# CIN kernel: the V2 matmuls moved ahead of a product row, and all six writes of M issued from ScalarE

## The chip, the cores and the metric

The kernel runs on one core of a Trainium2 chip. The metric is the device time of one execution in microseconds (us); the times given for a kernel are those of several executions, and their median. The profile is of one execution.

The engines are named as in the profile: PE is TensorE (matmuls), PEld its weight loads, DVE is VectorE, ACT is ScalarE, POOL is GpSimd, SP is SyncE. "SPq" and "ACTq" are the instruction streams of SP and ACT where they issue DMAs.

## The reference

A compressed interaction network of three layers over `x` of shape (1024, 64, 16), that is batch B, feature F, embedding E. Each layer multiplies `x` with the layer before it, feature by feature, and contracts the 64 x 64 products with a weight:

```python
x0 = x
h = x
for i in range(3):
    z = jnp.einsum('bfe,bge->bfge', x0, h).reshape(B, 64 * fh, E)
    y = jnp.einsum('oc,bce->boe', Ws[i], z) + bs[i][None, :, None]
    if i != 2:
        x_i, h = y[:, :64], y[:, 64:]
    else:
        x_i, h = y, y
    xs.append(x_i)
out = jnp.sum(jnp.concatenate(xs, axis=1), axis=2) @ fc_w.T + fc_b
```

The last layer is only summed against `fc_w`, so its weight can be folded: with V2[f,g] = sum over o of fc2[o] * W2[o,f,g], and M = V2 contracted with the second half of W1, the third layer's share is a form in x, x and h1. Both h1 and this form ("q") are then contractions of the same products x_f * x_g, h1 with weights from W0, q with weights from M.

## The kernel before

**Tiles.** The batch is cut into 32 chunks of 32 rows; a chunk has N = 32 * 16 = 512 columns, and features lie along the partitions. A chunk's products are made as four "rows" j = 0 to 3. A row is one block `z` of 128 x 2048: `product(c, j)` multiplies `xa[c]` (four shifted copies of x, 128 x 4 x 512) with `xb[c][j]` (x shifted by the row's offset). Most rows are made on DVE (L240, 2.2 us each), some on POOL. `half_contract(c, j, ...)` then runs four matmuls for each row named, with the left half of `w_all` (the h1 weights), into the PSUM tile of chunk c. One such matmul shows as two records of PE.

**The head.** The first four chunks c0, c1, c2, c3 are chunks 2, 3, 0 and 1. Only their h1 half is contracted at first, since the right half of `w_all` (the q weights) comes from M, which the kernel computes itself at this point:

- V2: eight matmuls (L359) of `fv2` (fc2, broadcast) with the two halves of W2, into two PSUM tiles `pv`. DVE transposes each (L364), and DVE (L371) and ACT (L372) copy the result into `v2t`.
- M: eight matmuls (L387) of `v2t` with W1 into four PSUM tiles `pm`; ACT copies them into the block `m_sb` (L401).
- M goes to DRAM, into `md`, by six DMAs: two of 512 KB (L416, one from each half of the partitions), two of 256 KB (L419, L420), one of 32 KB (L421) and one of 28 KB (L422). They are called write 1 to write 6 below. In the kernel before, write 1 and writes 3 to 6 are issued by SP and write 2 by ACT.
- M is read back skewed, as rows (L469, `read_rows`) and columns (L463, `read_columns`), into the block `ms`: of the first row's reads one half of the partitions by SP, the other by ACT; the columns of rows 1 to 3 by SP alone. DVE adds rows and columns into the right half of `w_all` (L499, `q_weights(j)`).
- Then 32 matmuls (L281, `head_q_tile`) run the kept products of chunks 0 and 1 through the q weights, and everything after is driven by a list.

**What sets the order.** The kernel is under a manual schedule: each engine runs its instructions in the order in which the code issues them, and the later part of the kernel sorts a list of (time, job) pairs by hand-given times before issuing it. Waits are semaphore waits put in by the framework. DMAs take one of eight completion semaphores in turn, whichever engine issues them, and an issue waits until the semaphore's DMA before it has landed. Order in the code around the change, for the engines concerned:

- PE: the last columns of c0 (L257), row 0 of c1 (L248), V2 (L359), rows 3 and 1 of c1, M (L387), `pcx` (L396), row 2 of c1, rows 0 to 3 of c2, rows 0, 3, 1, 2 of c3 (L248), then L281.
- DVE: rows of c0, rows 0 and 1 of c1, the two transposes (L364), two copies (L371), row 2 of c1, rows 0 to 3 of c2, rows 0, 1, 2 of c3, then L499.
- ACT: two copies of `v2t` (L372), the copy of `xb` for row 3 of c2 (L398), the four copies of M (L401), write 2 (L416), the copies of `xb` for rows 0 and 1 of c3 (L430), `cx` (L432), h1 of c1 (L268, L269), six copies of x for the kept chunks (L175 to L177), its three reads of M (L469, L463, L469), h1 of c2 and of c3.
- SP: the loads of x and weights up to c3, `linear` (L343), writes 1 and 3 to 6, its reads of M, `va` (L493), the loads of chunks 4 and 5.

Of the kernel before, what the change touches and what calls it, by code (L numbers as in the profile page):

```python
# [42 lines left out]
F = 64  # L43
# [27 lines left out]
def cin_kernel(ctx, tc, xra, xrb, wh, w0r, w1h, w2t, wx1, wx0, vec, lin, out):  # L71
    nc = tc.nc
# [19 lines left out]
    def used(n, times=1):  # L92
        left[n] -= times
        assert left[n] >= 0
        if left[n] == 0:
            vacant.append(n)
# [21 lines left out]
    for base in (0, 64, -64):  # L118
        nc.gpsimd.affine_select(
            out=shift, in_=shift, compare_op=ALU.not_equal, fill=1.0, base=base,  # L120
# [65 lines left out]
    c0, c1, c2, c3 = HEAD  # L186
# [49 lines left out]
    def product(c, j, first=0, last=NI, engine=nc.vector, uses=1):  # L236
        if first == 0:
            zs[c, j] = take(uses)
        at = slice(first, last)
        engine.tensor_tensor(  # L240
            blocks[zs[c, j]][:, at, :], xas[c][:, at, :],
            xbs[c][j].unsqueeze(1).to_broadcast([128, last - first, N]), ALU.mult,
        )

    def half_contract(c, *js, last=None):
        for j in js:
            for i in range(NI):
                nc.tensor.matmul(  # L248
                    accs[c][halves[i % 2]], w_all[:, j * NI + i, 0:64], blocks[zs[c, j]][:, i, :],
                    start=(j == 0 and i < 2), stop=(j == last and i > 1),  # L250
                )
            used(zs[c, j])
# [70 lines left out]
    for i in range(NI):  # L323
# [20 lines left out]
        out=linear, in_=bass.AP(tensor=lin.tensor, offset=lin.offset, ap=[[0, 128], [1, 384]])  # L344
# [2 lines left out]
    product(c1, NJ - 1, engine=nc.gpsimd)  # L347
    for j in (0, 1):
        product(c1, j)
    half_contract(c1, 0)  # L350


    v2b = take()
# [18 lines left out]
        nc.scalar.copy(v2t[halves[1 - h], at], v2q[halves[h]])  # L372
    used(v2b)
    product(c1, 2)
    half_contract(c1, 3, 1)


    mb = take()
# [29 lines left out]
    row = EXT * F  # L408

    def m_ap(f1, f2, dims):  # L410
        return bass.AP(tensor=md.tensor, offset=md.offset + f1 * row + f2 * F, ap=dims)

    m_rows = m_sb.rearrange("p m c -> p (m c)")

    for half, queue in enumerate((nc.sync, nc.scalar)):
        queue.dma_start(  # L416
            out=m_ap(0, 32 * half, [[row, F], [1, 32 * F]]), in_=m_rows[halves[half]]
        )
    nc.sync.dma_start(out=m_ap(64, 32, [[row, 32], [1, 32 * F]]), in_=m_rows[64:96])  # L419
    nc.sync.dma_start(out=m_ap(32, 64, [[row, 32], [1, 32 * F]]), in_=m_rows[32:64])  # L420
    nc.sync.dma_start(out=m_ap(64, 64, [[row, 32], [1, 4 * F]]), in_=m_rows[0:32, 0 : 4 * F])  # L421
    nc.sync.dma_start(  # L422
        out=m_ap(64, 68, [[row, 4], [4 * F, 7], [1, 4 * F]]),
        in_=m_rows[0:4, 4 * F :].rearrange("p (k c) -> p k c", c=4 * F),
    )
# [695 lines left out]
```

## Time and profile before

| | |
|---|---|
| median of 3 runs | 448.4 us (447.93, 448.40, 448.61) |
| the profiled execution | 448.52 us, of which the profile's span covers 446.7 |
| PE busy | 441.9 us, 99% of the span |
| DVE busy | 393.5 us, 88% |
| POOL busy | 366.7 us, 82% |
| ACT busy | 117.2 us, 26% |
| DMA | 99.85 MB, mean 224 GB/s |

How to read it: the profile gives the start and the length of each instruction on each engine, and for an engine that sat idle the releaser, the event that ended the wait. Times count from the start of the span. A timeline merges neighbouring instructions of one kind into one line: the start of the first, the time that they took together, the line of the code, the tile written and those read, and the count. PE's records overlap, since matmuls are pipelined: two records of L248 start every 0.43 us and each is listed with about 0.59 us.

### The profile page before, as it was taken

The numbers are of one execution on the slowest core, as the hardware profiler recorded it, in microseconds if no ns is written. First come the engines' busy times: TensorE is split into PE (matmuls) and PEld (weight loads), VectorE is DVE, ScalarE is ACT, GpSimd is POOL, SyncE is SP. The second block draws the span as 40 slices with busy tenths as digits, with TensorE's granted clock in tenths as the row PEclk, the third lists the DMA queues.
The fourth block names the chain that finished last, engine by engine and source line by source line (L and its number), as shares of the span: only waits on it lengthen the run. The fifth ranks groups of instructions, "written<-read, shape, count | busy, mean of one in ns | idle before, by whom it ended". The sixth has DMA issues, their size and how long they took to land.

```text
span 446.7 us, 5944 instructions
## 1 busy us (share of the span) xinstructions
PE 441.9 (99%) x2234; PEld 151.8 (34%) x2234; DVE 393.5 (88%) x293; ACT 117.2 (26%) x215; POOL 366.7 (82%) x128
## 2 busy tenths in 40 slices
PE   9999999999999999999999999999999999999997
PEld 5333333333333333333333333333333333333345
DVE  4897699989989989999899979999899998999644
ACT  3163241332223123131312212231231313123211
POOL 5424788998997979799797979979797997979910
PEclk9999999999999999999999999999999999999999
DMA  8996998397949597694949769494976949692400
GB/s 299 416 343 151 331 412 342 93 346 133 357 117 295 167 221 273 137 360 102 303 158 234 268 128 357 105 312 149 232 264 133 372 92 286 223 240 86 98 1 0
DMA packets 35060, 99.85 MB, mean 224 GB/s; under 512 B 6389, under 2 KB 7189, under 8 KB 28441
## 3 DMA queue, kind: packets, MB, share of 16 engines
q1 hardware_dynamic: 32376, 84.90, 53.7%
q0 software_dynamic: 1872, 13.63, 17.4%
q10 hardware_dynamic: 784, 0.95, 0.8%
q8 instruction: 17, 0.28, 0.2%
q14 instruction: 11, 0.08, 0.0%
HBM read 84.20 MB, written 1.64 MB: 192 GB/s over the span
## 4 chain that ended last, share of the span: by engine, by line
PE 91%; DMA 6%; DVE 1%; SPq 0%; issue 0%; DVEq 0%
PE alpha L530 45%; PE delta L530 20%; PE beta L530 11%; PE acc L530 7%; PE q L530 3%; DMA xa<-in_xra 3%; PE acc L281 3%; DMA xb<-in_xrb 2%; PE acc L248 2%; DMA z<-in_w0r 1%; DVE z L240 1%; PE y L530 0%; SPq L145 0%; SPq L195 0%; PE hx L530 0%
## 5 line engine op out<-in xcount | busy, mean ns | idle before, releaser
L661 POOL TENSOR_TENSOR z<-z,z 128x2048 f32<-128x2048 f32 (+1 forms) x78 | 299.9, 3878 | 28.8 <-PE alpha L530 28.8
L530 PE MATMUL alpha<-z,ws 128*64 128x512 f32 x624 | 235.4, 593 | 0.0
L644 DVE TENSOR_TENSOR z<-xa,xp 128x2048 f32<-128x2048 f32 x103 | 231.5, 2279 | 1.2
L530 PEld LDWEIGHTS alpha<-z,ws 128*64 128x64 f32 x624 | 72.4, 137 | 91.0 <-issue 90.5
L530 PE MATMUL delta<-z,w_all 128*64 128x512 f32 x208 | 96.5, 592 | 0.0
L530 PE MATMUL alpha<-z,w_all 128*64 128x512 f32 x208 | 93.4, 593 | 0.0
L530 PE MATMUL beta<-z,w_all 128*64 128x512 f32 x208 | 92.7, 594 | 0.0
L530 PE MATMUL delta<-z,ws 128*64 128x512 f32 x208 | 91.4, 592 | 0.0
L558 ACT COPY xp<-xb 128x512 f32<-128x512 f32 x88 | 51.4, 587 | 127.4 <-DVE z L644 109.2
L240 DVE TENSOR_TENSOR z<-xa,xp 128x2048 f32<-128x2048 f32 (+1 forms) x29 | 45.5, 1619 | 4.3 <-ACT xp L558 3.2
L240 POOL TENSOR_TENSOR z<-xa,xb 128x2048 f32<-128x2048 f32 x6 | 28.2, 4760 | 17.5 <-DMA xb<-in_xrb 17.5
L530 PEld LDWEIGHTS delta<-z,w_all 128*64 128x64 f32 x208 | 28.4, 137 | 32.2 <-issue 32.2
L530 PEld LDWEIGHTS alpha<-z,w_all 128*64 128x64 f32 x208 | 28.1, 137 | 32.0 <-issue 29.5
L530 PEld LDWEIGHTS delta<-z,ws 128*64 128x64 f32 x208 | 28.5, 137 | 27.4 <-issue 25.7
L530 PEld LDWEIGHTS beta<-z,w_all 128*64 128x64 f32 x208 | 28.0, 137 | 27.4 <-issue 27.4
L530 PE MATMUL acc<-z,w_all 128*64 128x512 f32 x128 | 28.1, 592 | 0.0
L248 PE MATMUL acc<-z,w_all 128*64 128x512 f32 x96 | 21.6, 597 | 1.1 <-DVE z L240 1.1
L675 ACT ACTIVATE snap<-alpha,vs 64x512 f32<-64x512 f32 x13 | 8.9, 684 | 50.2 <-PE alpha L530 50.2
L682 DVE SCALAR_TENSOR_TENSOR snap<-alpha,vs,snap 64x512 f32<-64x512 f32 x13 | 9.7, 747 | 12.5 <-PE alpha L530 12.5
L672 ACT COPY snap<-alpha 64x512 f32<-64x512 f32 x13 | 7.6, 581 | 49.2 <-PE delta L530 34.9
L305 DVE TENSOR_REDUCE acc<-uu 128x64 f32<-128x1024 f32 (+2 forms) x19 | 19.6, 1036 | 0.2
L650 DVE TENSOR_TENSOR xp<-xp,xb 128x512 f32<-128x512 f32 x26 | 18.2, 699 | 0.8
(121 smaller groups left out, 357.6 us busy)
## 6 DMA issues: line engine op xcount, KB each, us to landing
xa<-in_xra SPq DMA_DIRECT2D x32, 1024.0 KB, 8.9
xb<-in_xrb SPq DMA_DIRECT2D x128, 256.0 KB, 8.5
z<-z POOLq DMA_DIRECT2D x13, 1024.0 KB, 8.1
e<-in_xra SPq DMA_DIRECT2D x28, 128.0 KB, 8.2
xx<-in_xra SPq DMA_DIRECT2D x28, 128.0 KB, 2.5
z<-in_w2t SPq DMA_DIRECT2D x2, 1024.0 KB, 8.4
z<-in_wx SPq DMA_DIRECT2D x2, 1024.0 KB, 9.9
xa<-in_xra SPq DMA_DIRECT2D x5, 256.0 KB, 4.3
```

The lines of the kernel that those rows point to most:

```text
L240: engine.tensor_tensor(blocks[zs[c, j]][:, at, :], xas[c][:, at, :], xbs[c][j].unsqueeze(1).to_broadcast([128, last - first, N]), ALU.mult,)
L248: nc.tensor.matmul(accs[c][halves[i % 2]], w_all[:, j * NI + i, 0:64], blocks[zs[c, j]][:, i, :], start=(j == 0 and i < 2), stop=(j == las ...
L281: nc.tensor.matmul(accs[c][halves[1 - c % 2]], w_all[:, t, 64:128], blocks[zs[c, j]][:, i, :], start=(t == 0), stop=False, skip_group_chec ...
L305: nc.vector.tensor_reduce(acc[rows, of, k, half], uu[rows, of if at is None else at, E * half.start : E * half.stop].rearrange("p k (b e) ...
L530: nc.tensor.matmul(out, w, rhs, start=start, stop=stop, skip_group_check=True)
L558: nc.scalar.copy(bank, xbs[c][j])
L644: engine.tensor_tensor(blocks[b], xas[c], xbs[c][j].unsqueeze(1).to_broadcast([128, NI, N]), ALU.mult)
L650: nc.vector.tensor_tensor(bank, bank, xbs[p["b"]][j], ALU.add)
L661: nc.gpsimd.tensor_tensor(*(blocks[b][:, first:last] for b in (o, x, y)), ALU.subtract if in1 == "T3" else ALU.add,)
L672: nc.scalar.copy(snaps[0][p["O"]], alpha(p))
L675: nc.scalar.activation(snaps[1][p["O"]], alpha(p), AF.Identity, bias=bh1[p["A"]])
L682: nc.vector.scalar_tensor_tensor(hb_, alpha(p), bh1[p["A"]], hb_, ALU.add, ALU.add)
```

## The change

Two edits. The matmuls of c1's row 0 are taken from ahead of V2 and put behind it, so that PE runs V2 right after c0's columns and then rows 0, 3 and 1 of c1. And all six writes of M are issued by ACT, one after the other, where SP issued five of them.

```diff
@@ -347,7 +347,6 @@
     product(c1, NJ - 1, engine=nc.gpsimd)
     for j in (0, 1):
         product(c1, j)
-    half_contract(c1, 0)
...
@@ -372,7 +371,7 @@
     used(v2b)
     product(c1, 2)
-    half_contract(c1, 3, 1)
+    half_contract(c1, 0, 3, 1)
...
@@ -412,14 +411,14 @@
-    for half, queue in enumerate((nc.sync, nc.scalar)):
-        queue.dma_start(
+    for half in range(2):
+        nc.scalar.dma_start(
             out=m_ap(0, 32 * half, [[row, F], [1, 32 * F]]), in_=m_rows[halves[half]]
         )
-    nc.sync.dma_start(out=m_ap(64, 32, [[row, 32], [1, 32 * F]]), in_=m_rows[64:96])
-    nc.sync.dma_start(out=m_ap(32, 64, [[row, 32], [1, 32 * F]]), in_=m_rows[32:64])
-    nc.sync.dma_start(out=m_ap(64, 64, [[row, 32], [1, 4 * F]]), in_=m_rows[0:32, 0 : 4 * F])
-    nc.sync.dma_start(
+    nc.scalar.dma_start(out=m_ap(64, 32, [[row, 32], [1, 32 * F]]), in_=m_rows[64:96])
+    nc.scalar.dma_start(out=m_ap(32, 64, [[row, 32], [1, 32 * F]]), in_=m_rows[32:64])
+    nc.scalar.dma_start(out=m_ap(64, 64, [[row, 32], [1, 4 * F]]), in_=m_rows[0:32, 0 : 4 * F])
+    nc.scalar.dma_start(
         out=m_ap(64, 68, [[row, 4], [4 * F, 7], [1, 4 * F]]),
         in_=m_rows[0:4, 4 * F :].rearrange("p (k c) -> p k c", c=4 * F),
     )
```

In the changed kernel every line from L350 on has a number lower by one. On ACT the six writes stand where write 2 stood: behind the copies of M and ahead of the copies of `xb` for c3. The counts of matmuls, products, copies and DMAs are the same. Some blocks `z` change places, since row 0 of c1 is released later: the reads of M land in a block that held W2, no longer in the one of c1's row 0.

## The prediction

> **What bounds the kernel now.** I read the page's busy times first.
>
> ```profile
> PE 441.9 (99%) x2234; PEld 151.8 (34%) x2234; DVE 393.5 (88%) x293; ACT 117.2 (26%) x215; POOL 366.7 (82%) x128
> ```
>
> PE is busy in all but 4.8 of 446.7 us. So only what makes PE wait, or takes a wait away, can move the end, and the waits lie in the first 43 us. The timeline of PE there:
>
> ```profile
> 17.56 1.94 PE L248 MATMUL acc<-z,w_all 128*64 128x512 f32 x8 [0.83 <-DVE z L240]
> 19.43 1.92 PE L359 MATMUL pv<-z,fv 128*32 128x512 f32 x16
> ...
> 26.80 8.88 PE L248 MATMUL acc<-z,w_all 128*64 128x512 f32 x40
> 35.94 7.09 PE L248 MATMUL acc<-z,w_all 128*64 128x512 f32 x32 [0.26 <-DVE z L240]
> 42.85 13.90 PE L281 MATMUL acc<-z,w_all 128*64 128x512 f32 x64
> ```
>
> The reader is to see two things. PE idles 0.83 us before c1's row 0, for a product of DVE. And at 35.94, c3's row 0, it waits for DVE again; from there it never stops, so 35.94 is the moment that sets the end. What set it is in the timeline of DVE:
>
> ```profile
> 20.56 1.57 DVE L364 STREAM_TRANSPOSE z<-pv 128x512 f32<-128x512 f32 x2 [0.95 <-PE pv L359]
> 22.17 0.40 DVE L371 COPY res<-z 64x32 f32<-64x32 f32 x2
> 22.59 2.29 DVE L240 TENSOR_TENSOR z<-xa,xp 128x2048 f32<-128x2048 f32 x1
> 24.80 6.69 DVE L240 TENSOR_TENSOR z<-xa,xb 128x2048 f32<-128x2048 f32 x3
> 31.41 6.68 DVE L240 TENSOR_TENSOR z<-xa,xp 128x2048 f32<-128x2048 f32 x3
> 38.00 2.29 DVE L240 TENSOR_TENSOR z<-xa,xb 128x2048 f32<-128x2048 f32 x1
> 40.81 0.43 DVE L499 TENSOR_TENSOR w_all<-z 128x256 f32<-128x256 f32 x1 [0.53 <-DMA z<-md]
> ```
>
> From 20.56 to 40.29 DVE has no gap; a row costs 2.23 us. The group at 31.41 is c2's row 3 and c3's rows 0 and 1, so c3's row 0 runs from 33.64 to 35.9, and PE starts on it at 35.94. The one gap ahead of that is 0.95 us, for V2. The chain of waits names a DMA as the releaser of the product at 31.41, then 1.49 us of "issue"; DVE's own line shows it busy then, so I follow DVE. Last, who issues the writes of M, SP and ACT:
>
> ```profile
> 28.13 0.52 SPq L416 DMA_DIRECT2D md<-z  x1
> 28.70 0.57 SPq L419 DMA_DIRECT2D md<-z  x1
> 29.31 1.94 SPq L420 DMA_DIRECT2D md<-z  x1
> 31.30 2.16 SPq L421 DMA_DIRECT2D md<-z  x1
> 33.50 1.54 SPq L422 DMA_DIRECT2D md<-z  x1
> 36.84 0.47 SPq L469 DMA_DIRECT2D z<-md  x1
> ```
>
> ```profile
> 28.13 0.55 ACTq L416 DMA_DIRECT2D md<-z  x1
> 28.73 1.11 ACT L430 COPY xp<-xb 128x512 f32<-128x512 f32 x2 [0.62 <-DMA xb<-in_xrb]
> ...
> 36.94 0.49 ACTq L469 DMA_DIRECT2D z<-md  x1
> 37.53 1.08 ACTq L463 DMA_DIRECT2D z<-md  x1
> ```
>
> The first three writes cost their issuer 0.52 to 0.57 us, writes 4 to 6 cost 1.94, 2.16 and 1.54, though they are the smaller ones: SP is held from 28.13 to 35.04. That is nothing to SP, which has to wait for M to land anyway. ACT instead goes on at once: its copies for c3's rows 0 and 1 follow at 28.73.
>
> [...]
>
> **The change, part by part.**
>
> *V2 first.* PE is free of c0 at about 16.7 (17.56 less 0.83). W2's second half has landed by 16.94: SP's issue that waits for it stands at 16.96. V2 takes four steps of 0.43, so it ends near 18.8 and DVE, done with c1's row 1 at 19.61 (20.56 less 0.95), finds it ready. The 0.95 us vanish, and every DVE row up to c2's row 3 is 0.95 earlier; that one ends at 33.64 − 0.95 = 32.69. If W2 came late, 0.8 us would be the cover. c1's row 0 then costs nothing where it is: PE runs it from 18.9, rows 3 and 1 until 23.7, and M from there, 1.06 us earlier than at 24.86.
>
> *M is not earlier for that.* ACT's copy L398 stands ahead of the copies of M and waits for a DMA until 25.43; the copies then run from 26.05 to 28.10. Neither edit touches this load. The writes begin at 28.13 as before.
>
> *Six issues on ACT.* Unknown: how long ACT is held. Lower end: six times 0.55, with 0.05 between, is 3.6 us, free at 31.7. Upper end: every issue from the third on takes the mean of the three slow ones, (1.94 + 2.16 + 1.54) / 3 = 1.88 us, so 28.13 + 2 × 0.60 + 4 × 1.93 = 37.1. Below the lower end nothing speaks. I take what SP shows: the slow issues come free at 31.25, 33.46 and 35.04, as if by the progress of the earlier writes, and the order of the six is the same. ACT is free at 35.05.
>
> *Queued behind it.* First the copies for c3 (L430): 35.08 to 35.67 and to 36.2. c3's row 0 on DVE needs the first, so DVE, free at 32.69, waits until 35.73 and ends the row at 37.97; PE starts at 38.02. Before it was 35.94: +2.08. The early 0.95 is wasted, and what was hidden cover (copy ready at 29.3, wanted at 33.64) is gone. The point from which the change loses on this path is ACT free at 35.94 − 0.05 − 2.24 − 0.64 = 33.0. Rows 1 and 2 of c3 end at 40.2 and 42.4, PE wants them at 41.5 and 43.2. PE is through c3 at 42.85 + 2.08 = 44.93.
>
> *Then ACT's half of the reads.* From L430 to the last L177, ACT works without a gap from 28.73 to 34.93, 6.2 us. So its reads are issued from 35.05 + 6.2 = 41.3, not 36.94. From the start of its L463 to DVE's first L499 it was 40.81 − 37.53 = 3.28 us; if 0.6 lies between the starts of the two reads again, DVE gets the first row at 41.9 + 3.28 = 45.2, perhaps 0.5 earlier with SP's reads out of the way, and with 0.43 for L499 PE starts at 45.1 to 45.6. I take 45.25, which is 42.85 + 2.4.
>
> *SP.* It loses 6.9 us of issuing that only filled a wait, a gain of nothing. But the load of chunk 4 takes a semaphore that ACT's last read had, so it is held until that lands, near 46, against 43.98: 2 us late. In the trace chunk 4's first row is on DVE from 51.76 and PE wants it at 56.59, a slack of 2.5; PE being 2.4 late too, the slack stays. POOL and the q weights of rows 1 to 3 move by about as much. Nothing behind 45 absorbs PE's delay, since PE has no idle there.
>
> *Sum.* −0.95 on DVE, regained and lost again; +2.08 by the copy; +0.3 by the reads: +2.4 on the profiled execution's 448.52, of which 446.7 is the span and 1.8 lies around it, so 450.9. That execution lies 0.1 above the median of 448.4; in medians I forecast 450.8, 450.0 to 451.8 for this case alone (ACT free at 34.4 to 35.6, reads 0 to 0.6).
>
> **The rivals.**
>
> *The hold stays with SP (not slower).* If the slow issues come from what SP's queue had outstanding, the loads of c3 and `linear` of before, ACT is free at 31.7, its second copy at 32.9; DVE isn't held, and c3's row 0 is 0.95 early. PE is at L281 at 41.9, ACT's reads start at 37.9 and DVE has row 0 between 41.2 and 41.8, so PE starts near 42.1: 447.6 to 447.9. For it: ACT's own write at 28.13 took 0.55. Against: 32 and 28 KB are still slow at 31.30 and 33.50, when those loads are over or nearly so. It decides below ACT free at 33.0.
>
> *Worse.* Writes that fall into a running write are all slow, write 3 included (before, it was issued 0.6 us behind write 1). ACT is free at 37.1, 2 us later, and all follows: 452.8.
>
> *In between.* One slow issue: ACT free near 33, copies just in time, reads from 39.2, so PE at L281 at 42.9 to 43.4: 448.7.
>
> *V2 not ready.* If V2 waited for W2 until after 17.8, part of the 0.95 would stay. It changes only the second rival, since in the first case the 0.95 is lost anyway.
>
> **How the numbers follow.** My case 0.63, the hold with SP 0.15, worse 0.13, in between 0.09. About 0.2%, 0.9 us, is what a measurement of this kernel can tell from no change; so 447.5 to 449.3 is "same". Slower: 0.63 + 0.13 = 0.76. The hold with SP and the case in between lie inside "same" mostly, 0.15; faster, if more than 0.9 is kept of the gain, 0.09. The range leaves out the hold with SP (0.15) and the end of "worse" (0.04): 448.0 to 452.7.
>
> **What would show it.** PE: V2 at about 16.8 with the 0.83 gone; DVE: transposes at 19.6, then a wait of about 3 us for ACT ahead of c3's row 0. ACT: three issues near 0.55, three of 1.5 to 2.2, copies at 35.1, reads at 41.3. PE: c3's row 0 at 38.0 and L281 at 45.2. I am wrong if the late issues on ACT are short, or if PE shows L281 at or ahead of 42.85.

## The result and the profile after

The changed kernel takes 453.9 us (median of 6 executions, 452.84 to 454.72), the kernel before 448.5 (6 executions, 447.67 to 449.01): a ratio of 1.0121, 95% interval 1.0101 to 1.0141. It is slower, as forecast, but by 5.4 us where the prediction said 2.4, and 453.9 lies above its range of 448.0 to 452.7. The profiled execution took 452.95 us, its span 451.2, against 448.52 and 446.7 before: 4.5 us more in the span.

The timeline of PE in the changed kernel (start, length, line, tiles; in brackets the idle time ahead and who ended it):

```profile
16.11 1.94 PE L358 MATMUL pv<-z,fv 128*32 128x512 f32 x16
...
38.96 8.61 PE L248 MATMUL acc<-z,w_all 128*64 128x512 f32 x32 [4.29 <-DVE z L240]
47.41 13.90 PE L281 MATMUL acc<-z,w_all 128*64 128x512 f32 x64
```

V2 runs first, and neither PE's 0.83 us ahead of c1's row 0 nor DVE's 0.95 for V2 is left. Then c3's row 0 starts at 38.96, 3.02 us later than the 35.94 of before. And the same 32 records, which took 7.09 us before, take 8.61: another 1.52. Together that is 4.54, and L281 starts 4.56 later, and the whole span is 4.5 longer. So between these two profiles nothing after 47.41 adds to the delay or takes from it. Against a second profile of the kernel before (the last experiment) c3's row 0 starts 3.95 us later and L281 5.48, while the span is 4.2 longer, so that about 1.3 us are absorbed further on: a split to a tenth of a microsecond holds for one pair of executions only.

Who keeps PE waiting is in the timelines of DVE and of ACT:

```profile
23.79 6.70 DVE L240 TENSOR_TENSOR z<-xa,xb 128x2048 f32<-128x2048 f32 x3 [0.95 <-DMA xb<-in_xrb]
...
36.62 4.49 DVE L240 TENSOR_TENSOR z<-xa,xp 128x2048 f32<-128x2048 f32 x2 [3.94 <-ACT xp L429]
```

```profile
28.43 1.17 ACTq L415 DMA_DIRECT2D md<-z  x2
29.64 1.93 ACTq L418 DMA_DIRECT2D md<-z  x1
31.62 2.11 ACTq L419 DMA_DIRECT2D md<-z  x1
33.77 1.22 ACTq L420 DMA_DIRECT2D md<-z  x1
35.03 0.92 ACTq L421 DMA_DIRECT2D md<-z  x1
36.00 1.11 ACT L429 COPY xp<-xb 128x512 f32<-128x512 f32 x2 [7.59 <-DMA md<-z]
...
39.30 0.48 ACTq L468 DMA_DIRECT2D z<-md  x1
39.68 0.61 ACT L177 COPY xx<-xa 64x512 f32<-64x512 f32 x1
```

DVE has done c2's row 3 at 32.68 and then waits. The chain is the forecast one: ACT issues writes from 28.43 to 35.95, its copy for c3's row 0 comes at 36.00, DVE waits 3.94 us for it, PE waits 4.29 for DVE. Two details differ. Only the first two issues are short (1.17 for both); the third, a short one on SP before, takes 1.93. And ACT's first read of M is issued at 39.30, amid the copies of x (L175 to L177, the last ends at 42.2), not behind them.

The 1.52 us are TensorE's clock. The windows view of the changed kernel, in which the column behind POOL is the granted clock:

```profile
core 0: us, PE busy (x) PEld busy (x) DVE busy (x) ACT busy (x) POOL busy (x), PEclk, DMA share, GB/s
34.00:39.00 5.00, 0.71 (x6) 0.04 (x2) 2.38 (x2) 2.96 (x6) 3.82 (x9) 0.97 0.48 130
39.00:42.00 3.00, 3.00 (x8) 0.96 (x10) 3.00 (x2) 2.94 (x6) 0.00 (x0) 0.50 0.64 156
42.00:43.00 1.00, 1.00 (x6) 0.28 (x4) 1.00 (x1) 0.59 (x2) 0.00 (x0) 0.96 0.60 128
```

From 39 to 42 PE is busy without a gap and runs at half its clock: 8 records in 3 us, where at full clock, two every 0.43 us, there would be 14. Spread over the rows, the time at half clock is 0.03 × 5 / 0.5 + 3.0 + 0.04 × 1 / 0.5 = 3.4 us. The kernel before has a mean clock of 1.0 in nearly every execution; there PE never idles over 0.83 us in this stretch.

### The profile page after: what moved, and what is told of

It is laid out like the page before. It is cut to its first block, busy times and chain, and to the rows that moved or that the text cites. A ratio compares the mean times of both kernels' runs of the same rounds, so it can differ in the third digit from the quotient of the medians.

```text
span 451.2 us, 5943 instructions
## 1 busy us (share of the span) xinstructions
PE 442.8 (98%) x2234; PEld 151.5 (34%) x2234; DVE 394.2 (87%) x293; ACT 117.2 (26%) x215; POOL 365.6 (81%) x128
## 4 chain that ended last, share of the span: by engine, by line
PE 91%; DMA 6%; SPq 1%; ACT 1%; DVE 1%; issue 0%; ACTq 0%
PE alpha L529 45%; PE delta L529 20%; PE beta L529 10%; PE acc L529 7%; PE q L529 3%; PE acc L281 3%; DMA xb<-in_xrb 3%; PE acc L248 2%; DMA xa<-in_xra 2%; DMA md<-z 1%; DVE z L240 1%; SPq L145 0%; PE y L529 0%; ACT z L400 0%; SPq L195 0%
## 5 line engine op out<-in xcount | busy, mean ns | idle before, releaser
L529 PE MATMUL acc<-z,w_all 128*64 128x512 f32 x128 | 28.1, 592 | 0.0
L248 PE MATMUL acc<-z,w_all 128*64 128x512 f32 x96 | 23.2, 632 | 4.5 <-DVE z L240 4.5
L649 DVE TENSOR_TENSOR xp<-xp,xb 128x512 f32<-128x512 f32 x26 | 18.2, 699 | 0.8
```

Source lines behind the costliest of these rows:

```text
L248: nc.tensor.matmul(accs[c][halves[i % 2]], w_all[:, j * NI + i, 0:64], blocks[zs[c, j]][:, i, :], start=(j == 0 and i < 2), stop=(j == las ...
L529: nc.tensor.matmul(out, w, rhs, start=start, stop=stop, skip_group_check=True)
L649: nc.vector.tensor_tensor(bank, bank, xbs[p["b"]][j], ALU.add)
```

## The experiments

The theory after this result: six issues in a row hold ACT, its copies for c3 come late, and the PE idle time that follows is paid twice, once as delay and once as half clock. The rivals: V2's place does it; the accumulator buffers or the late M hold PE, not the copies; the half clock has another cause than the idle; the hold belongs to ACT as an issuer.

### V2 first alone

The changed kernel with the writes issued as before (five by SP, one by ACT).

```diff
-    for half in range(2):
-        nc.scalar.dma_start(
+    for half, queue in enumerate((nc.sync, nc.scalar)):
+        queue.dma_start(
...
-    nc.scalar.dma_start(out=m_ap(64, 32, ...
+    nc.sync.dma_start(out=m_ap(64, 32, ...
```

> The changed kernel with the writes of M issued as before (write 2 by ScalarE, the other five by SyncE): the V2 edit alone. Theory (the loss is all in ScalarE's six issues): the copies for c3 follow one write, near 29, VectorE has no wait ahead of c3's row 0, PE starts that row 0.8 to 1.1 us earlier than before (about 34.9) and the time is 447.4 to 447.9, 0.6 to 1.1 us below the kernel before. Rival (the order of V2 and row 0 has a cost of its own, for instance a later h1 of c1 or a later M): 448.5 or more.

Measured: 448.48 us (22 executions) against 448.61, ratio 0.9999 (0.9985 to 1.0013). V2 first is no loss, and no gain either: the 447.4 to 447.9 expected did not come. The median is at the edge of the rival's 448.5, but a cost of the new order is not seen in the profile (of the shortest of the 22 executions, 447.29 us). There DVE has no wait ahead of c3's row 0, and PE none from the end of V2 to L281, which starts at 41.62; V2 itself waits 0.81 us for the second half of W2. But most of V2's 0.95 us is lost at the next row of DVE, which now waits for a load, as in the changed kernel above:

```profile
23.55 6.70 DVE L240 TENSOR_TENSOR z<-xa,xb 128x2048 f32<-128x2048 f32 x3 [0.93 <-DMA xb<-in_xrb]
```

### The writes alone

The kernel before with all six writes on ACT, V2 where it was.

```diff
-    for half, queue in enumerate((nc.sync, nc.scalar)):
-        queue.dma_start(
+    for half in range(2):
+        nc.scalar.dma_start(
...
-    nc.sync.dma_start(out=m_ap(64, 32, ...
+    nc.scalar.dma_start(out=m_ap(64, 32, ...
```

> The kernel before with all six writes on ScalarE, V2 where it was: the queue edit alone. Theory: ScalarE is held to about 36, VectorE starts c3's row 0 at 36.6 whether or not it was early, PE resumes at 38.9 to 39.0, after an idle of 3.4 to 3.6 us instead of 4.3. Without a slower clock after it that gives +3.0 us, 451.5; with the half clock for one or two stretches of 3.2 us, 453.0 to 454.7; so 451.5 to 454.7, and above the kernel before by at least 3. Rival (the two edits hurt each other, since V2 first lengthens the gap that PE falls into): 450 or less.

Measured: 453.03 us (6 executions), ratio 1.0089 (1.0064 to 1.0113). The profile is the changed kernel's: ACT is free at 35.82, c3's row 0 on PE

```profile
38.78 8.56 PE L248 MATMUL acc<-z,w_all 128*64 128x512 f32 x32 [4.08 <-DVE z L240]
```

and L281 at 47.18. The writes carry 4.4 of the 5.4 us, and the rival, in which the two edits hurt each other, falls. The last 1 us is not explained for certain: the two intervals overlap, and none of these six executions has the longer half clock (mean clock 0.992) that three of six have in the changed kernel. One of the six took 451.18 us with the clock at 1.0; no profile shows whether PE idled less in it.

### Sixteen filler matmuls ahead of c3's row 0, then eight

If the half clock comes from PE's idle time, matmuls in that time keep the clock up. They write into c3's accumulators, which the first true matmul starts anew. Sixteen in the first, eight in the second:

```diff
     new_acc(c3)
+    for n in range(16):
+        nc.tensor.matmul(
+            accs[c3][halves[n % 2]], w_all[:, 0, 0:64], xas[c2][:, 0, :], start=True, stop=True
+        )
```

> The changed kernel with 16 more matmuls (3.4 us at full clock) on PE between c2's last row and c3's row 0, into c3's own accumulator, which c3's first real matmuls overwrite; the result is unchanged. They fill most of the time in which PE waits. Theory (half clock follows from the idle of 4.3 us): PE still resumes c3's row 0 near 39.0, but at full clock, 0.43 us a pair; L281 starts near 45.9 instead of 47.4, the granted clock is 1.00, and the time is 451.0 to 451.7, all runs close together, about 2.4 us below the changed kernel's median. Rival (the clock drop has another cause, for instance the sudden start or the chip's state): 453 to 455 as the changed kernel, clock 0.992 to 0.996.

Measured: 454.4 us (5 executions), ratio 1.012 (1.0097 to 1.0143). The time expected was missed, since I had sized a filler too small: the sixteen took 7.04 us, 34.62 to 41.49, so c3's row 0 started 2.5 us later than in the changed kernel. But it ran in 7.04 us and the clock was 1.0 in all five. Eight were tried next:

> As the fill before, with 8 more matmuls instead of 16: the run before showed that one takes 0.43 us, so that 16 took 6.9 us and held c3's row 0 until 41.5 by themselves. 8 take 3.4 us and end near 38, ahead of the product that PE waits for. Theory (half clock follows from PE's idle of 4 us): c3's row 0 starts near 39.0 as in the changed kernel, at full clock; granted clock 1.00; L281 near 45.9 instead of 47.4; 451.3 to 452.2, which is the 454.4 of the longer fill less the 2.5 us that it came later. Rival (another cause of the lower clock): clock 0.992 to 0.996, 453 to 455.

```profile
34.66 3.60 PE L483 MATMUL acc<-xa,w_all 128*64 128x512 f32 x16
38.69 7.09 PE L248 MATMUL acc<-z,w_all 128*64 128x512 f32 x32 [0.43 <-DVE z L240]
```

Measured: 451.19 us (4 executions), ratio 1.0064 (1.0049 to 1.0079), clock 0.999 to 1.0; the time is a tenth below the range expected. The wait for ACT is the same, c3's row 0 starts at nearly the same time (38.69), and its 32 records take 7.09 us, as before. Work that nobody needs makes the kernel shorter: what is left against the kernel before, measured beside it, is 451.19 − 448.16 = 3.0 us, where the changed kernel had 5.4. This splits the loss: about 3.0 for the delay of PE, 2.4 for the clock.

### The copies for c3 ahead of the six writes

```diff
+    for j in (0, 1):
+        xb3 = ps.tile([128, N], F32, tag="y", name=f"xp_{c3}_{j}")
+        nc.scalar.copy(xb3, xbs[c3][j])
+        xbs[c3][j] = xb3
     m_rows = m_sb.rearrange("p m c -> p (m c)")
...
-    for j in (0, 1):
-        xb3 = ps.tile([128, N], F32, tag="y", name=f"xp_{c3}_{j}")
-        nc.scalar.copy(xb3, xbs[c3][j])
-        xbs[c3][j] = xb3
```

> The changed kernel with ScalarE's two copies of xb for c3 moved ahead of the six writes; the rest of ScalarE's work stays behind them. Theory in its simple form (only these copies matter): VectorE has no wait ahead of c3's row 0, PE starts it near 34.9, and the time is 447.5 to 449. Rival: c3's accumulator is the PSUM buffer of c1's, which ScalarE reads (L268, L269) behind the writes, so that PE is held all the same until these are done, 37.1 + 0.2 + 1.3, near 38.7; then PE resumes at 38.6 to 38.9, waits for ScalarE instead of VectorE, and the time is 452.5 to 454.5.

Measured: 452.01 us (11 executions, 450.38 to 456.99), ratio 1.0087 (1.0054 to 1.012). Neither time came. That the copies are what c3 waits for is confirmed, and the rival with the accumulator buffers falls: PE starts c3 at 35.23. But now M is late:

```profile
45.00 13.96 PE L281 MATMUL acc<-z,w_all 128*64 128x512 f32 x64 [2.69 <-DVE w_all L498]
```

The writes start at 29.95 and end on ACT at 37.5, 1.5 us later than in the changed kernel; the reads start at 40.67, over 3 us later than there (37.21), and L281 waits 2.69 us for the q weights. So the writes' issue is itself on a path that sets the end, and what stands ahead of them counts as well as what stands behind; why the reads lose more than the 1.5 us isn't shown. PE's clock stays at 1.00 after this wait, though it is longer than others that halved it (see below). This profiled execution, the longest of the eleven, also waits 3.2 us far later, for the DMA with which POOL adds one block to another.

### All six on SP

V2 first, and all six writes on the other queue.

```diff
-        nc.scalar.dma_start(
+        nc.sync.dma_start(
...
-    nc.scalar.dma_start(out=m_ap(64, 32, ...
+    nc.sync.dma_start(out=m_ap(64, 32, ...
```

> The changed kernel with all six writes issued by SyncE instead of ScalarE, in the same order. Theory: the slow issues belong to six writes in a row and not to ScalarE: SyncE shows the same lengths (two issues near 0.6, then about 1.9, 2.1, 1.3, 0.9) and is held to about 36, which costs nothing, since it waits for M anyway; ScalarE's copies for c3 follow at 28.8; PE has no wait ahead of c3's row 0; 447.5 to 448.7, the same as with V2 alone. Rival (six writes on one queue land M later, and that costs too): the q weights are late, L281 waits, 449.5 or more.

Measured: 448.71 us (18 executions, 447.37 to 453.0), ratio 1.0022 (1.0004 to 1.004), which is 1.0 us above the kernel before where the changed kernel is 5.4 above it. Two more executions, not in these numbers, took 454.55 and 454.73 with a mean clock of 0.996. The issues on SP are as long as on ACT:

```profile
28.56 1.15 SPq L415 DMA_DIRECT2D md<-z  x2
29.76 1.85 SPq L418 DMA_DIRECT2D md<-z  x1
31.65 2.06 SPq L419 DMA_DIRECT2D md<-z  x1
```

Writes 5 and 6 follow with 1.37 and 0.73, up to 35.89. So the hold belongs to six writes in a row, not to ACT. What ACT adds is what queues behind it. The small rest, 1.0 us, fits this profile, in which M is read late (from 38.98) and L281 starts at 43.87 after 1.78 us of idle. The view names ACT's copy L269 as what ended that wait; it stands behind ACT's reads of M and ended at 43.74, and the q weights, from the same reads, at 43.72. So of the two expectations the rival's came in part. Why M is read late here isn't settled, and the executions above 452 us have no profile.

### Three or four on ACT, the rest on SP

Writes 4 to 6, or 5 and 6, moved to SP.

```diff
-    nc.scalar.dma_start(out=m_ap(32, 64, ...
+    nc.sync.dma_start(out=m_ap(32, 64, ...
...
```

> The changed kernel with writes 1 to 3 on ScalarE and 4 to 6 on SyncE: half the dose. Theory: PE's start on c3's row 0 is ScalarE's free time plus 2.96 us (36.00 to 38.96 in the changed kernel) or PE's own end of c2's rows near 34.5, whichever is later. With three issues (0.6, 0.6, 1.9) ScalarE is free near 31.6, so the copies are ready in time; PE has at most 0.5 us of wait and the time is 447.7 to 448.9. Rival (whatever is queued on ScalarE is held until the writes have landed, however few): 451 or more.

> The changed kernel with writes 1 to 4 on ScalarE and 5 and 6 on SyncE. By the same rule: ScalarE is free near 33.8, PE starts c3's row 0 near 36.7, after an idle of about 2 us[...] (granted clock 1.00); the time is 1.7 to 2.3 us above that with three writes, 449.8 to 451. Rival (the loss comes in a step once the copies are late, the clock with it): 452.5 or more and clock below 0.998; or no loss yet, 448.5.

With four, 451.19 us (4 executions), ratio 1.0065 (1.0049 to 1.0082). ACT is free at 34.11, PE starts c3 at 37.08, 2.97 later, after 1.94 us of idle:

```profile
37.08 8.78 PE L248 MATMUL acc<-z,w_all 128*64 128x512 f32 x32 [1.94 <-DVE z L240]
```

The clock fell in all four by their mean of 0.996 (one has a profile), which I had not expected at so short an idle.

With three, ACT is free at 32.39, c3 starts at 35.36 (again 2.97 later) and L281 at 42.28, earlier than in the kernel before: on this path there is no loss left. Yet the four executions, one of them with the clock at 1.0, took 453.52 us in the median (450.7 to 455.55), ratio 1.0112 (1.0069 to 1.0155). In the profiled one, which took 455.55, the waits of PE past 100 us show where:

```profile
PE delta L529 <- DMA z<-z: 4.9, 1, 4.9
```

The DMA with which POOL adds one block to another (L658) was issued at 105.8 and landed 12.9 us later; in the kernel before, the thirteen of them land 6.9 to 8.7 us after their issue. That PE wait, too, was followed by half clock, until 123.6. Why it landed late here isn't settled, and the other three executions have no profile. So the rule on PE's start held in both. Of the times, the one with four came 0.2 us above its range of 449.8 to 451, with half clock in it that had not been counted, and the one with three missed.

### The small writes first

All six on ACT, in the order 32 KB, 28 KB, 256, 256, 512, 512.

```diff
-    for half in range(2):
-        nc.scalar.dma_start(
-            out=m_ap(0, 32 * half, [[row, F], [1, 32 * F]]), in_=m_rows[halves[half]]
-        )
...
+    for half in range(2):
+        nc.scalar.dma_start(
+            out=m_ap(0, 32 * half, [[row, F], [1, 32 * F]]), in_=m_rows[halves[half]]
+        )
```

> The changed kernel, all six writes still on ScalarE, in another order: 32 KB, 28 KB, 256, 256, 512, 512 KB. Theory (an issue is held until the write two places ahead of it is nearly out, so that the bytes of the first four set the hold): the last issue is released when 572 of the 1084 KB are out, at about 150 KB/us from 29 that is 32.8; ScalarE is free near 33, PE starts c3's row 0 near 36 after an idle of 1 to 1.5 us; 449 to 450.5, 3.5 to 5 us below the changed kernel. Rival (each issue that falls into a running write costs about 1.9 us, whatever its size and place): ScalarE is free near 36, 453 to 455 as the changed kernel.

Measured: 449.94 us (12 executions, 448.22 to 453.34), ratio 1.0038 (1.0014 to 1.0063). The same six writes, the same queue, 4 us less. The 32, 28, 256 and 256 KB took 0.34, 0.48, 0.31 and 0.44 us, the two of 512 together 1.77. ACT's copies come at 31.82, c3 on PE at 35.11, L281 at 42.03. So it is what lies ahead of a write on its queue that makes its issue long, neither the number of writes nor the engine. The time lies in the expected range, but partly by luck: expected was a PE wait of 1 to 1.5 us, and the profile (448.36 us) has one of 0.26, as in the kernel before. What the executions of 449.7 us and more lose, three of them with the clock at 0.996, no profile shows.

### A row of c2 on POOL

V2 first with the writes as before, to make something of V2's gain: the product of c2's row 3 on POOL, its copy on ACT gone.

```diff
-    xb2 = ps.tile([128, N], F32, tag="set", name=f"xp_{c2}_{NJ - 1}")
-    nc.scalar.copy(xb2, xbs[c2][NJ - 1])
-    xbs[c2][NJ - 1] = xb2
...
-        product(c2, j, uses=1 + NI)
+        product(c2, j, uses=1 + NI, engine=nc.gpsimd if j == NJ - 1 else nc.vector)
```

> V2 first, the writes of M as in the kernel before, and in addition the product of c2's row 3 on GpSimd, which is idle from 17 to 31, instead of VectorE (its copy on ScalarE falls away). Theory (until L281 PE is bound by VectorE's rows, then by the q weights): c3's row 0 is ready 2.2 us earlier, PE has no wait from V2 on, ends c3's rows near 41.3 and then waits for M's first row, which is there at 41.2; 447.2 to 448.2, up to 1 us below the kernel before. Rival (what bounds behind 45, GpSimd's chain and the loads, gives it back): 448.2 to 449, the same.

Measured: 457.38 us (5 executions), ratio 1.0195 (1.0179 to 1.021), the longest of all; both expectations missed. DVE's three rows of c2 take 15.36 us, not 6.7:

```profile
23.81 15.36 DVE L240 TENSOR_TENSOR z<-xa,xb 128x2048 f32<-128x2048 f32 x3 [0.67 <-DMA xb<-in_xrb]
```

Two of them take 6.6 us each, while POOL runs its products of 4.55 and 5.98 us, all with both operands in SBUF. The row that ran ahead of POOL's first product took 2.29. A second operand in PSUM shows no such loss: in the kernel before, DVE's three rows with the copies `xp` took 6.68 from 31.41 on, while POOL ran a product from 30.67 to 35.93. By my estimate from these lengths, one waits for about the whole of the other: 6.6 − 2.29 = 4.3 us more for a DVE row, against a POOL product of 4.55. PE then waits 2.71 and 2.95 us, and both times its clock halves.

### Both kernels once more

A second profile of each, to see what varies.

> The kernel before once more, for a second profile of it. Theory (the head's start differs from execution to execution, so that the 0.4 us which the first profile showed between the landing of c2's first xb and VectorE's need of it are no fixed number): VectorE starts c2's row 0 between 23.7 and 24.8 and c0's last columns start on PE between 12.2 and 13.1. Rival (the first profile is typical): 24.7 to 24.9 and 13.0 to 13.1.

> The changed kernel once more, for a profile that may show the longer of its two kinds of execution. Theory (a clock of 0.992 is two stretches of half clock in a row behind the same idle of PE): PE starts c3's row 0 near 39 and either 3.2 us (clock 0.996, L281 near 47.4) or 6.6 us (0.992, L281 near 49.1) are at half clock there, and PE waits nowhere later. Rival (the second stretch belongs to another wait, further on): L281 near 47.4 also at 0.992, and a wait of PE behind 60.

The kernel before took 448.75 us, and both starts lie in the ranges expected (c0's last columns at 12.36). c2's row 0 starts on DVE at 23.87 instead of 24.80, c3's on PE at 35.01, L281 at 41.93, all about 0.9 earlier than in the first profile; and the span is 447.0, not shorter than 446.7. PE lost the 0.9 again at POOL's accumulating DMA:

```profile
PE delta L530 <- DMA z<-z: 0.9, 1, 0.9
```

So the start of the head varies by nearly a microsecond between executions, and a head that is early by that much is no earlier at the end.

The changed kernel took 453.94 us with a mean clock of 0.992. c3 starts at 39.07 after 4.27 us of idle, much as in its first profile, but L281 only at 48.40, 1 us later. PE waits nowhere further on, so the rival falls. Its windows:

```profile
36.00:38.00 2.00, 0.00 (x0) 0.00 (x0) 1.27 (x1) 1.88 (x4) 1.90 (x8) 0.78 0.21 72
38.00:42.00 4.00, 2.93 (x8) 1.01 (x10) 4.00 (x3) 3.91 (x8) 0.04 (x1) 0.50 0.56 137
42.00:44.00 2.00, 2.00 (x6) 0.47 (x4) 1.42 (x1) 1.58 (x3) 0.00 (x0) 0.51 0.62 149
```

Here the half clock lasts 0.22 × 2 / 0.5 + 4 + 0.49 × 2 / 0.5 = 6.8 us, from 37.1 to 44.0, twice the 3.4 of the first profile. Its first 2 us fall into PE's idle and cost nothing, which is why L281 comes ahead of the 49.1 expected. Three of the changed kernel's six executions have a mean clock of 0.996 and take 452.84 to 453.55 us, three have 0.992 and take 454.26 to 454.72: 3.4 us at half clock is 0.004 of the span, 6.8 us is 0.008.

## Why the prediction was right in sign and wrong in size

The chain came as forecast: the writes hold ACT, its copy for c3 is late, DVE waits for the copy and PE for DVE. The step that failed is the sum. "+2.08 by the copy" takes PE's wait at its own length and puts the clock behind the wait at nothing, without a reason; the half clock cost another 1.52 us in the first profile and 2.42 in the second. The hold of ACT was also sized 0.95 us too short, and the 0.3 for the reads did not come.

*V2 first: "The 0.95 us vanish".* They do at V2, and 0.95 of wait for c2's `xb` takes their place at 23.79. The prediction carried the 0.95 through to c2's rows and did not ask when their load lands. The profile of before shows no wait there, but that execution had a late head (c2's row 0 at 24.80, against 23.87 in the second profile). W2, too, was read from that one profile: in six of the later ones V2's second half waits 0.6 to 1.2 us for it, until 17.8 to 18.2. No wait of DVE follows from that, since its transposes stand behind c1's products. For the changed kernel it made no difference, as the prediction said: the gain is lost at the copies anyway.

*M is not earlier.* Right: the writes begin at 28.43, against 28.13.

*"ACT is free at 35.05".* It is 36.00, between the case taken and "worse" (37.1). 0.3 is the later start. The other 0.65 is about one short issue more: six writes hold ACT for 7.52 us (28.43 to 35.95), five held SP for 6.91, and writes 3 to 6 took 6.18 us together against 6.21 before. The prediction let SP's last issue end the hold and left no room for a sixth. Among the four the lengths moved: write 3 took 1.93 us and not 0.57, writes 5 and 6 took 1.22 and 0.92, not 2.16 and 1.54. The profile of before had the clue to write 3. "The first three writes cost their issuer 0.52 to 0.57 us" was read over two engines, and it was the first two on SP and one on ACT: per queue, two large ones went short and the third was long. All six on one queue make write 3 the third.

*Queued behind it: PE 2.97 us after ACT is free.* Right to a few hundredths, in every profile where it was the bound: 36.00 to 38.96, 34.11 to 37.08, 32.39 to 35.36. With ACT at 36.00 the delay is 3.02 instead of 2.08.

*The reads, +0.3.* Zero. The prediction queued ACT's reads behind its copies of x. In the trace the read at 39.30 is issued while copies ahead of it in the code are still to run, until 42.2. So on ACT a DMA issue can go out while compute instructions that stand ahead of it in the code have yet to finish, five of them here. L281 found the q weights ready.

*The term that was missing: PE's clock.* The wait cost 1.52 us more than its length in the first profile and 2.42 in the second (c3 to L281 9.33 us, against 6.91 before). This is the largest part of the miss: 450.9 forecast for the profiled execution + 0.95 for ACT + 1.5 for the clock − 0.3 for the reads = 453.05, and it took 452.95. The median lies about 1 us higher because half of the executions have the longer half clock. The fillers show that the idle is its cause: the same delay without the idle runs at full clock (0.999 to 1.0 in all nine executions with fillers). The half clock lasts 3.4 us in the first profile and 6.8, twice as long, in the second. In the experiment with a row of c2 on POOL the clock falls twice:

```profile
30.00:33.00 3.00, 0.30 (x2) 0.29 (x4) 3.00 (x2) 2.94 (x7) 2.46 (x2) 0.94 1.04 256
36.00:38.00 2.00, 0.27 (x2) 0.00 (x0) 2.00 (x1) 0.00 (x0) 2.00 (x2) 0.99 0.06 12
38.00:40.00 2.00, 0.78 (x4) 0.24 (x6) 2.00 (x2) 0.00 (x0) 2.00 (x1) 0.86 0.72 183
42.00:44.00 2.00, 2.00 (x10) 0.55 (x8) 2.00 (x2) 0.00 (x0) 0.00 (x0) 0.79 0.47 106
```

Worked out as above, the half clock lasts from 32.6 to 36.0 and from 39.4 to 42.8: the four edges are 3.4 us apart. In the first profile of the changed kernel the clock falls 0.3 us before PE resumes and is at half for 3.4 us; in the second it falls 1.95 us before and is at half for 6.8. What decides between the two lengths isn't shown.

Nor is it shown how much idle it takes. 1.94 us were enough (four executions of four by their mean clock of 0.996, one of them profiled). But 2.69 us were not with the copies ahead of the writes (42.31 to 45.00), where the clock reads 1.00 from 42 to 60.

*"Nothing behind 45 absorbs PE's delay".* True between the two first profiles: L281 +4.56, span +4.5. For a PE that is early it is not: 0.9 us were given back at POOL's DMA in the second profile of before. So the rival "the hold stays with SP", had its hold been right, would hardly have earned its 0.95 either; with V2 first alone, where ACT is free as in that rival, the time was 448.48.

Of the rivals, "worse" had the right mechanism in half (write 3 is long), without the clock; its 452.8 comes near by luck, since a hold 1.1 us too long stands in for the clock. "The hold stays with SP" is wrong in its reason: SP's loads had nothing to do with it, since the same lengths stand on either queue.

## What to carry to other kernels

Before moving DMA issues to a compute engine, ask for each what lies ahead of it on that queue, and what the engine's next instruction feeds: several large writes in a row hold the issuer for microseconds (six held ACT for 7.52 us here), and putting the small ones first, or leaving the row to an idle SP, took away most of the loss here (ratios of 1.0038 and 1.0022, against 1.0121). Where a TensorE stall reaches 1.94 us, the shortest that halved the clock here, allow for half clock behind it: it cost 1.5 to 2.4 us beyond the stall in this case, though one stall of 2.69 us cost nothing more. If the wait can't be removed, try matmuls that fill it. Take a slack of under 1 us from two profiles, not from one.

## What the runs showed of the hardware

- Issue times of writes to DRAM, in the order of each queue (KB: us). Before, SP 512: 0.52, 256: 0.57, 256: 1.94, 32: 2.16, 28: 1.54, and ACT 512: 0.55. Six on ACT, 512 and 512: 1.17, 256: 1.93, 256: 2.11, 32: 1.22, 28: 0.92. With three on each, ACT 512 and 512: 1.59, 256: 2.32, while on SP 256: 0.34, 32: 0.37, 28: 0.56 at the same time. Write 3 (256 KB), with 1024 KB issued ahead of it, took 0.57 us where these were split between two queues and 1.93 where all were on its own. So the hold goes by the queue. Whether it is the bytes ahead or something else about these writes that makes an issue long isn't separated by any run here.
- TensorE's clock halved after idles of 1.94 to 4.85 us, for 3.4 or 6.8 us. With a row of c2 on POOL, where it halved twice, the four edges lay 3.4 us apart. It did not halve after 0.43 and 1.78 us, nor after one idle of 2.69.
- DMAs of POOL that accumulate landed 6.9 to 8.7 us after their issue in the kernel before. One took 12.9 in another run, with no cause found; PE waited 4.9 us for it.
- A product on DVE with both operands in SBUF took 6.6 us beside one on POOL, and 2.29 ahead of it. Three with one operand in PSUM took 6.68 in the kernel before, from 31.41 on, with one on POOL until 35.93.
